# Four graph layers on one core: sharing single tiles of exponentials between ScalarE and VectorE

## The chip, the core and the metric

The kernel runs on one core of a Trainium2 chip. TensorE (PE in the profile) multiplies matrices, ScalarE (ACT) evaluates functions such as the exponential, VectorE (DVE) does elementwise arithmetic and reductions, GpSimd (POOL) copies and starts some of the transfers, SyncE (SP) starts most of them. The engines run side by side and wait for each other through semaphores. Matrix products land in PSUM, a small memory of eight banks; everything else lives in SBUF. The metric is device time of one execution in microseconds (us).

## What is computed

Four layers follow each other on a graph of N = 3327 nodes with D = 128 features. Nearly all of the time is in the first, an attention with 128 "heads" (one for each of the d = 128 rows of the reshaped q, k and v) of depth 8, whose scores get the adjacency matrix added twice:

```python
q = (x @ Wq.T).reshape(d, n, h)          # d = 128, n = 3327, h = 8; k and v alike
a = jnp.einsum('dnh,dmh->dnm', q, k) * d ** -0.5
a = a + adj + adj
a = jax.nn.softmax(a, axis=2)
out = jnp.einsum('dnm,dmh->dnh', a, v).reshape(n, h * d) @ Wo.T
x = layernorm(x + out)
```

So 128 x 3327 x 3327 exponentials are needed. The other layers are products with the adjacency matrix: one scaled by the inverse roots of its row sums, one with rows divided by row sums plus the transpose divided by column sums, and one plain, each with a residual and a layer norm.

## The kernel before

**Tiling of the attention.** The queries are cut into seven columns of CW = 476, the keys into 26 tiles of 128, and these into four key blocks KBS of 7, 7, 6 and 6 tiles, called here kb 0 to 3. A block of work is one column with one key block: 28 blocks, taken column by column with kb 0 to 3 inside. In a block the 128 heads d run in 32 groups of four (GROUP).

**One step.** For one head, `exponents` (line 616) is called three times, for the three sets of SETS: 3, 2 and 2 key tiles where the block has 7, and 2, 2 and 2 where it has 6. A set si has score banks `sc[si]` of its own (3 + 2 + 2 of PSUM's 8 banks). TensorE writes one 128 x 476 product for each tile (line 632; the added adjacency comes in through the operands), then an engine reads the whole set out of PSUM and writes the exponentials to `e` in SBUF. That is ScalarE with one activation for the set (line 640), except for the last set of a group's first head in most groups (`on_vector`, line 454): that whole set is done on VectorE by `vector_exp` (line 590). Over the kernel 784 sets of two tiles go to VectorE, 9,968 to ScalarE.

**The exponential on VectorE.** Line 596 reads PSUM, clamps, and scales into an integer whose upper bits are an exponent. Lines 597 and 599 split it by bit operations into a power of two and a mantissa. Five operations of line 602 then evaluate a polynomial of degree five (Horner's rule, the last one multiplies by the power). The first of these eight is issued at once, the others are kept in the list `vec`.

**The weighing.** One group later, `weigh` (line 647) multiplies the exponentials with the values: for one key tile r, four heads side by side, summed over the key block in the eighth bank `o`. PLACES, FIRST and FULL say after which of the twelve sets of a group each of the 6 or 7 weighings stands. After three groups `flush` (line 665) adds `o` into `acc` on VectorE.

**Order.** The attention is written with a manual schedule: the order of instructions on TensorE, ScalarE, GpSimd and VectorE is that of the program text. VectorE's kept operations are placed by `vector_work` (line 607), which has a clock for ScalarE (0.95 or 0.84 for each set) and one for VectorE, and takes operations from `vec` as long as VectorE's clock is behind. In a spare moment the adjacency matrix is transposed in 91 pieces of 512 x 256 (`piece_work`, line 213), whose row sums and column sums are taken on VectorE too: a transpose and three reductions, in two bursts, in every eighth group. `copy_queries` (line 513) prepares the next group's queries on VectorE where kb is 0.

**After the attention.** `divide` (line 1119) normalises with GpSimd, and three gathers (`gather`, line 1098) multiply the transposed adjacency, loaded as one 128 x 26 x 128 tile `eT` for each row tile through a pool of five buffers, with the features.

Of the kernel before, what the change touches and what calls it, by code (L numbers as in the profile page):

```python
# [30 lines left out]
POLY = (-0.12145248055458069, 1.287218689918518, 0.8447736501693726, 0.7106341123580933, 0.24892811477184296)  # L31
# [19 lines left out]
def kernel(ctx: ExitStack, tc: tile.TileContext, x, adj, wq, wk, wv, wo,  # L51
# [83 lines left out]
    colsum = const.tile([P, T], F32, name="colsum")  # L135
# [20 lines left out]
    csum = const.tile([P, NP // 32], F32, name="csum")  # L156
# [56 lines left out]
    def piece_work(pool, u, c, ai):  # L213

        nj = PIECE // 32
        w = min(PIECE, N - c * PIECE)
        at = pool.tile([P, nj, 4, 32], F32, name="at")
        nc.vector.transpose(at.rearrange("p j t b -> p t j b"), ai.rearrange("p t (j a) -> p t j a", a=32))
        yield at
        if c == 0:  # L220
            maxima[u] = pool.tile([P, 4, NPC], F32, name="pmax")
            sums[u] = pool.tile([P, 4, NPC], F32, name="psum")
        nc.vector.tensor_reduce(maxima[u][:, :, c], ai[:, :, 0:w], AX.X, ALU.max)
        yield at
        nc.vector.tensor_reduce(sums[u][:, :, c], ai[:, :, 0:w], AX.X, ALU.add)
        yield at
        part = csum[:, c * nj:(c + 1) * nj]
        if u == 1:
            nc.vector.tensor_reduce(part, at.rearrange("p j t b -> p j (t b)"), AX.X, ALU.add)
        else:  # L230
            cs = pool.tile([P, nj], F32, name="cs")
            nc.vector.tensor_reduce(cs, at.rearrange("p j t b -> p j (t b)"), AX.X, ALU.add)
            nc.vector.tensor_tensor(part, part, cs, ALU.add)
        yield at

    def store_tops(pool, u, top, n):

        hi = pool.tile([P, 4], F32R, name="rhi")
        nc.vector.tensor_copy(hi, top)
        lo = pool.tile([P, 4], F32R, name="rlo")  # L240
        nc.vector.tensor_tensor(lo, top, hi.bitcast(F32), ALU.subtract)
        for row, sb in enumerate((hi, lo)):
            for i in range(P // n):
                nc.gpsimd.dma_start(out=flat_ap(lead_s[u], row * SUPER + i * P, [[1, n], [n, 4]]),
                                    in_=sb[n * i:n * i + n, :].bitcast(F32))
# [172 lines left out]
    def attention():  # L418
        with tc.tile_pool(name="ed", bufs=1) as ed, tc.tile_pool(name="kq", bufs=3) as kq, \
# [34 lines left out]
            def on_vector(kb, g):  # L454

                return g % 4 != 0 if kb == 0 else KBS[kb][1] == 7 or g % 8 != 0
# [5 lines left out]
            PLACES = {7: (1, 1, 4, 6, 8, 10, 10), 6: (0, 2, 4, 6, 8, 10)}  # L462
# [79 lines left out]
            loaded, worked, turning = [], [], []  # L542

            def background(n):
                if n % PACE == 2 and worked:
                    piece_store(pe, *worked.pop(0))
                if n % PACE == 2 and pieces:
                    u, c = pieces.pop(0)
                    loaded.append((u, c, piece_load(pe, u, c)))

            def background_work(n):
                if n % PACE == 4 and loaded:
                    u, c, ai = loaded.pop(0)
                    steps = piece_work(pe, u, c, ai)
                    worked.append((u, c, next(steps)))
                    next(steps)
                    clock[1] += 2.4
                    turning.append(steps)
                if n % PACE == 0 and turning:
                    clock[1] += 2.4  # L560
                    for _ in turning.pop():
                        pass

            def prepare(b, d):

                n = b * NHG + d // GROUP
                if d % GROUP == 0:
                    while any(of is None for _, of, _ in vec):
                        vec.pop(0)[2]()
# [12 lines left out]
                if n + 1 < len(groups) and blocks[groups[n + 1][0]][1] == 0 \  # L582
                        and d % GROUP == 1 - on_vector(blocks[b][1], d // GROUP):
# [6 lines left out]
            def vector_exp(e, x, of):  # L590


                y = ex.tile([P, 2, CW], F32, name="ey")
                t = ex.tile([P, 2, CW], F32, name="et")
                yi, ti = y.bitcast(I32), t.bitcast(I32)
                nc.vector.tensor_scalar(yi, x, -58 * math.log(2.0), 2 ** 24 / math.log(2.0), ALU.max, ALU.mult)  # L596
                vec.append((0.7, of, lambda: nc.vector.tensor_scalar(ti, yi, UPPER, EXPONENT, ALU.bitwise_and,  # L597
                                                                 ALU.bitwise_xor)))
                vec.append((0.7, of, lambda: nc.vector.tensor_scalar(yi, yi, LOWER, QUARTER, ALU.bitwise_and,  # L599
                                                                 ALU.bitwise_or)))  # L600
                for i, a in enumerate(POLY):
                    vec.append((1.2, of, lambda i=i, a=a: nc.vector.scalar_tensor_tensor(  # L602
                        e, e if i else y, a, t if i == len(POLY) - 1 else y, ALU.add, ALU.mult)))

            clock = [0.0, 0.0]

            def vector_work(b):

                while vec and clock[1] < clock[0]:
                    cost, _, step = vec.pop(0)  # L610
                    step()
                    clock[1] += cost
                clock[0] += 0.95 if KBS[blocks[b][1]][1] == 7 else 0.84
                clock[1] = max(clock[1], clock[0] - 1)

            def exponents(b, d, si):
# [19 lines left out]
                if on_vector(kb, d // GROUP) and (d % GROUP, si) == (0, 2):  # L636
                    vector_exp(e[:, 0:n, :], s[:, 0:n, 0:CW], (b, d // GROUP))
                    clock[1] += 1.2
                else:
                    nc.scalar.activation(e[:, 0:n, :], s[:, 0:n, 0:CW], AF.Exp, scale=2.0)  # L640
# [6 lines left out]
            def weigh(b, g, r):  # L647
# [6 lines left out]
                while any(of == (b, g) for _, of, _ in vec) and r >= SETS[len(queue_of)][2][0]:  # L654
                    vec.pop(0)[2]()
# [19 lines left out]
            def store(b, f):  # L675
                nb = min(PACK, NHG - f * PACK)
                for j in range(GROUP):
                    nc.gpsimd.dma_start(  # L678
# [6 lines left out]
            with tc.manual_schedule(engines={mybir.EngineType.PE, mybir.EngineType.Activation,  # L685
# [8 lines left out]
                for b, d in steps:  # L694
# [3 lines left out]
                    for si in range(len(SETS[KBS[blocks[b][1]][1]])):  # L698
                        vector_work(b)
# [335 lines left out]
    pick = act.tile([P, 32], F32, name="pick")  # L1035
    nc.vector.tensor_tensor(pick, ident[:, 0:32], ident[:, 32:64], ALU.add)
    nc.vector.tensor_tensor(pick, pick, ident[:, 64:96], ALU.add)
    nc.vector.tensor_tensor(pick, pick, ident[:, 96:128], ALU.add)
    ps = bank(7)
    nc.tensor.matmul(ps[0:32, 0:NP // 32], lhsT=pick, rhs=csum, start=True, stop=True)  # L1040
    for q in range(4):
        nc.vector.tensor_copy(colsum[32 * q:32 * q + 32, :],
                              ps[0:32, 0:NP // 32].rearrange("a (s q) -> a q s", q=4)[:, q, :])

# [17 lines left out]
    inv_col = inverse_degree(colsum, "inv_col")  # L1062
# [34 lines left out]

    def gather(t, y, col, b, meanwhile=()):
# [13 lines left out]
        for _, what in todo:  # L1112
            what()
        return ps
# [4 lines left out]
    def divide(t):  # L1119
# [7 lines left out]
        nc.gpsimd.tensor_tensor(ons[t][:n], o[:n, 0:H, :], rec[:n, :].unsqueeze(1).to_broadcast([n, H, D]), ALU.mult)  # L1127
# [38 lines left out]
    with tc.manual_schedule(engines={mybir.EngineType.PE, mybir.EngineType.SP}):  # L1166
# [18 lines left out]
        for t in range(T):  # L1185
# [9 lines left out]
            norm(n, h[:n, :], xs[1][:n, t, :])  # L1195

# [77 lines left out]
```

## Time and profile before

| what | value |
|---|---|
| time, median of 3 runs | 10,740.89 us (10,740.8 to 10,744.52) |
| the profiled execution | 10,739.45 us, its span 10,737.5 us |
| first to last exponential on ScalarE | 317.7 to 9,966.2 us |
| from there to the end | 771 us |
| ScalarE's activations, line 640 | 9,968, busy 9,360.0 us |
| VectorE's polynomial steps, line 602 | 3,920, busy 4,511.6 us |
| column sums, lines 229, 232 and 233 | busy 123.4 us |

The profile gives, for each engine, the time that its instructions took and, for each group of instructions, the idle time of the engine ahead of them and the instruction whose semaphore ended it. Busy times of the engines overlap: the share of one engine says nothing on the path. A matmul's end is modelled, so that a busy TensorE isn't one at its peak; the distance between the starts of its instructions says more. On ScalarE an activation's record lasts longer than its share of the pipeline: the next one starts 844 ns after a two-tile set and 1,241 ns after a three-tile set where nothing holds it up (medians of start to start), though their records last 1,016 and 1,402 ns on average.

### The profile page before, as it was taken

What the parts mean: (1) busy time and instruction counts of PE and PEld (TensorE: products, weight loads), DVE (VectorE), ACT (ScalarE), POOL (GpSimd) and SP (SyncE); (2) the same over time, 40 slices, a digit from 0 to 9 for tenths busy, and PEclk for the clock granted to TensorE, in tenths of its full rate; (3) what the DMA queues carried; (4) which work ended last, traced back from release to release, by engine and by line L of the source; (5) the groups of instructions that cost most, each with busy time, mean ns of one, the idle gap of its engine ahead of it and who ended that gap; (6) DMA issues with size and microseconds to landing.
All of it is one profiled execution on the core that took longest, in us unless ns stands there. A gap on an engine that the chain in (4) does not pass through costs nothing. (4 is left out here: it accounts for less than half of the span.)

```text
span 10737.5 us, 200822 instructions
## 1 busy us (share of the span) xinstructions
PE 10565.1 (98%) x76941; PEld 4105.8 (38%) x76941; DVE 7960.2 (74%) x8554; ACT 9584.8 (89%) x10447; POOL 1554.7 (14%) x2739
## 2 busy tenths in 40 slices
PE   8899999999999999999999999999999999999999
PEld 5333333333333333333333333333333333333779
DVE  6777888777888777887788777888777777777412
ACT  3899999999999999999999999999999999999400
POOL 0111121111221111211122110121111100001200
PEclk9999999999999999999999999999999999999999
DMA  7678886788876888768887588886888867788676
GB/s 270 181 184 188 209 210 181 181 192 201 213 188 171 198 201 209 190 166 200 198 211 196 156 191 191 199 199 172 193 195 202 193 162 179 181 189 196 219 283 246
DMA packets 1013760, 2116.43 MB, mean 197 GB/s; under 512 B 206759, under 2 KB 730985, under 8 KB 998979
## 3 DMA queue, kind: packets, MB, share of 16 engines
q1 hardware_dynamic: 932014, 1985.55, 74.4%
q0 software_dynamic: 79392, 116.16, 3.5%
q8 instruction: 623, 10.21, 0.4%
q14 instruction: 335, 2.74, 0.1%
q10 hardware_dynamic: 1396, 1.77, 0.1%
HBM read 1863.03 MB, written 239.54 MB: 196 GB/s over the span
## 5 line engine op out<-in xcount | busy, mean ns | idle before, releaser
L640 ACT ACTIVATE e<-sc 128x952 f32<-128x952 f32 (+1 forms) x9968 | 9360.0, 1085 | 312.1 <-PE sc L632 284.3
L658 PE MATMUL o<-e,v_pad 128*32 128x476 f32 (+1 forms) x46592 | 5647.1, 573 | 39.4 <-DVE acc L671 18.5
L632 PE MATMUL sc<-qt,kt 64*128 64x476 f32 x23296 | 4491.6, 440 | 52.9 <-ACT e L640 33.5
L632 PEld LDWEIGHTS sc<-qt,kt 64*128 64x128 f32 x23296 | 2184.3, 184 | 4433.6 <-ACT e L640 3740.6
L602 DVE SCALAR_TENSOR_TENSOR e<-e,ey 128x952 f32<-128x952 f32 x2352 | 2707.0, 1151 | 77.4
L596 DVE TENSOR_SCALAR ey<-sc 128x952 int32<-128x952 f32 x784 | 901.1, 1149 | 1411.5 <-PE sc L632 1389.9
L658 PEld LDWEIGHTS o<-e,v_pad 128*32 128x32 f32 (+1 forms) x46592 | 1035.2, 108 | 1907.4 <-issue 1885.1
L533 POOL COPY v_pad<-vs 128x192 f32<-128x192 f32 (+1 forms) x896 | 444.5, 522 | 8018.6 <-DMA vs<-v_img 6214.0
L602 DVE SCALAR_TENSOR_TENSOR e<-ey 128x952 f32<-128x952 f32 x784 | 903.4, 1152 | 27.2
L602 DVE SCALAR_TENSOR_TENSOR e<-e,et 128x952 f32<-128x952 f32 x784 | 901.2, 1149 | 22.3
L253 POOL DMA_DIRECT2D adjT_s<-at x1352 | 760.1, 570 | 132.7 <-DMA adjT_s<-at 92.6
L599 DVE TENSOR_SCALAR ey<-ey 128x952 int32<-128x952 int32 x784 | 519.7, 663 | 27.1
L597 DVE TENSOR_SCALAR et<-ey 128x952 int32<-128x952 int32 x784 | 518.3, 661 | 26.9
L1110 PE MATMUL bank<-y,eT 128*128 128x128 f32 (+1 forms) x4056 | 473.9, 276 | 0.4 <-DVE h L1232 0.4
L1110 PEld LDWEIGHTS bank<-y,eT 128*128 128x128 f32 (+1 forms) x4056 | 465.3, 192 | 5.7 <-DVE h L1232 0.6
L671 DVE TENSOR_TENSOR acc<-o,acc 128x476 f32<-128x476 f32 x231 | 150.3, 651 | 281.5 <-PE o L658 280.9
L517 DVE TENSOR_SCALAR qt<-qt 32x1428 fp32r<-32x1428 f32 x224 | 201.7, 900 | 103.2 <-DMA qt<-q_s 89.2
L519 DVE CAST qt<-qt 64x1904 fp32r<-64x1904 f32 x224 | 260.4, 1163 | 7.6
L1070 ACT ACTIVATE rstd<-mv,eps 128x1 f32<-128x1 f32 x104 | 30.4, 292 | 263.6 <-DVE mv L1068 263.6
L678 POOL DMA_DIRECT2D o_s<-acc x308 | 199.4, 651 | 35.4 <-DVE acc L671 20.8
L1213 PE MATMUL bank<-a,y 128*128 128x512 f32 (+2 forms) x364 | 145.5, 562 | 0.0
L362 ACT ACTIVATE hi<-pp 128x1024 fp32r<-128x1024 f32 x52 | 53.0, 1024 | 87.9 <-PE pp L308 86.3
(148 smaller groups left out, 2274.7 us busy)
## 6 DMA issues: line engine op xcount, KB each, us to landing
qt<-qimg SPq DMA_DIRECT2D x1344, 476.0 KB
kt<-k_s SPq DMA_DIRECT2D x5316, 96.0 KB
kt<-k_s SPq DMA_DIRECT2D x1762, 128.0 KB
eT<-adjT_s SPq DMA_DIRECT2D x78, 1664.0 KB
qimg<-qt SPq DMA_DIRECT2D x224, 476.0 KB
vs<-v_img SPq DMA_DIRECT2D x224, 224.0 KB
adjT_s<-at POOLq DMA_DIRECT2D x1352, 32.0 KB, 4.8
vs<-v_img SPq DMA_DIRECT2D x224, 192.0 KB
```

The lines of the kernel that those rows point to most:

```text
L253: nc.gpsimd.dma_start(out=flat_ap(adjT_s, (t * P + 32 * q) * NP + c * PIECE, [[NP, 32], [P, ns], [1, P]]), in_=at[32 * i:32 * i + 32].rear ...
L517: return [(0.9, None, lambda: nc.vector.tensor_scalar(qt[32:64, 1:], qf[0:32, 0:GROUP - 1], -1.0, None, ALU.mult)), (0.4, None, lambda: nc ...
L519: (1.2, None, lambda: nc.vector.tensor_copy(qt[64:128], qf[0:64]))]
L533: nc.gpsimd.tensor_copy(vp[:, 32:32 + nt * GROUP * 32].rearrange("p (x c) -> p x c", c=32)[:, :, 0:H], vs.rearrange("p (x c) -> p x c", c=H))
L596: nc.vector.tensor_scalar(yi, x, -58 * math.log(2.0), 2 ** 24 / math.log(2.0), ALU.max, ALU.mult)
L597: vec.append((0.7, of, lambda: nc.vector.tensor_scalar(ti, yi, UPPER, EXPONENT, ALU.bitwise_and, ALU.bitwise_xor)))
L599: vec.append((0.7, of, lambda: nc.vector.tensor_scalar(yi, yi, LOWER, QUARTER, ALU.bitwise_and, ALU.bitwise_or)))
L602: vec.append((1.2, of, lambda i=i, a=a: nc.vector.scalar_tensor_tensor(e, e if i else y, a, t if i == len(POLY) - 1 else y, ALU.add, ALU.m ...
L632: nc.tensor.matmul(s[:, i, 0:CW], lhsT=kt[64 * rg:64 * rg + 64, k, pos * P:(pos + 1) * P], rhs=qt[64 * rg:64 * rg + 64, k, :], start=False ...
L640: nc.scalar.activation(e[:, 0:n, :], s[:, 0:n, 0:CW], AF.Exp, scale=2.0)
L658: nc.tensor.matmul(o[32 * j:32 * j + 32, 0:CW], lhsT=values[b, g][:m, c:c + 32], rhs=es[b, g * GROUP + j, r][:m, :], start=(r == 0 and u = ...
L1110: nc.tensor.matmul(ps[:n, 0:D], lhsT=e[:m, s, :n], rhs=y[:m, s, col:col + D], start=(s == 0), stop=(s == T - 1))
```

## The change

Where VectorE took a whole set of two tiles, it now takes the second tile of twice as many sets; ScalarE does the other tile of such a divided set, and its activation is issued first. 1,554 sets are divided (48, 64, 55 and 55 in a block of kb 0, 1, 2 and 3), all spaced evenly: every 6th set in kb 1, about every 7th in kb 2 and 3. The polynomial has one coefficient fewer; both engines' exponentials carry a common factor, which PHASE sets and which the division takes out again. `vector_exp` keeps all but its first operation in `vec` as before, now 476 wide and with two buffers each for `y` and `t`. The two clocks get a cost for each size of activation, and VectorE's operations are taken only up to the time at which its next fixed duty (a divided set, or a flush) is due. The background work comes in three single steps that are taken where they fit. In 6-tile blocks the weighings stand after sets 1, 3, ..., 11 in place of 0, 2, ..., 10. Column sums are no longer taken from the pieces: in the second layer's gather each loaded `eT` is reduced and summed (`add_columns`). The very last stores of the attention go through the SyncE and ScalarE queues, and the first `divide` multiplies on VectorE.

```diff
-POLY = (-0.12145248055458069, 1.287218689918518, 0.8447736501693726, 0.7106341123580933, 0.24892811477184296)
+POLY = (-0.039287679561190725, 0.7694055213858888, 0.3602062482980112, 0.1471829588776368)
+PHASE = 0.7927868171488225 * math.log(2.0) / 2
...
         nc.vector.tensor_reduce(sums[u][:, :, c], ai[:, :, 0:w], AX.X, ALU.add)
         yield at
-        part = csum[:, c * nj:(c + 1) * nj]
-        if u == 1:
-            nc.vector.tensor_reduce(part, at.rearrange("p j t b -> p j (t b)"), AX.X, ALU.add)
-        else:
-            cs = pool.tile([P, nj], F32, name="cs")
-            nc.vector.tensor_reduce(cs, at.rearrange("p j t b -> p j (t b)"), AX.X, ALU.add)
-            nc.vector.tensor_tensor(part, part, cs, ALU.add)
-        yield at
...
-            def on_vector(kb, g):
-                return g % 4 != 0 if kb == 0 else KBS[kb][1] == 7 or g % 8 != 0
+            def on_vector(b, d, si):
+                kb = blocks[b][1]
+                p = 3 * d + si
+                if kb == 0:
+                    return p % 24 in (2, 11, 17)
+                if KBS[kb][1] == 7:
+                    return p % 6 == 2
+                return p % 7 == 2 and p % 12 != 9 or p % 7 == 3 and p % 12 == 10
...
-            PLACES = {7: (1, 1, 4, 6, 8, 10, 10), 6: (0, 2, 4, 6, 8, 10)}
+            PLACES = {7: (1, 1, 4, 6, 8, 10, 10), 6: (1, 3, 5, 7, 9, 11)}
...
+            def background(n):
+                if spare:
+                    return
...
                     steps = piece_work(pe, u, c, ai)
-                    worked.append((u, c, next(steps)))
-                    next(steps)
-                    clock[1] += 2.4
-                    turning.append(steps)
-                if n % PACE == 0 and turning:
-                    clock[1] += 2.4
-                    for _ in turning.pop():
-                        pass
+                    spare.extend([lambda: worked.append((u, c, next(steps))), lambda: next(steps), lambda: next(steps)])
...
             def vector_exp(e, x, of):
-                y = ex.tile([P, 2, CW], F32, name="ey")
-                t = ex.tile([P, 2, CW], F32, name="et")
+                while sum(to is not None for _, to, _ in vec) > len(POLY):
+                    take()
+                y = ex.tile([P, CW], F32, name="ey", bufs=2)
+                yi, parts = y.bitcast(I32), {}
                 nc.vector.tensor_scalar(yi, x, -58 * math.log(2.0), 2 ** 24 / math.log(2.0), ALU.max, ALU.mult)
...
-                    vec.append((1.2, of, lambda i=i, a=a: nc.vector.scalar_tensor_tensor(
-                        e, e if i else y, a, t if i == len(POLY) - 1 else y, ALU.add, ALU.mult)))
+                    vec.append((0.69, of, lambda i=i, a=a: step(i, a)))
...
-            def vector_work(b):
-                while vec and clock[1] < clock[0]:
-                    cost, _, step = vec.pop(0)
-                    step()
-                    clock[1] += cost
-                clock[0] += 0.95 if KBS[blocks[b][1]][1] == 7 else 0.84
-                clock[1] = max(clock[1], clock[0] - 1)
+            COST = (0.0, 0.455, 0.85, 1.265)
+            def next_fixed(b, d, si):
+                at, nt = clock[0], KBS[blocks[b][1]][1]
+                for _ in range(12):
+                    if on_vector(b, d, si):
+                        return at + COST[SETS[nt][si][1] - 1] + 0.15
+                    if 3 * (d % GROUP) + si == 11 and (d // GROUP % PACK == PACK - 1 or d == D - 1):
+                        return at + 0.3
+                    at += COST[SETS[nt][si][1]]
+                    ...
+            def vector_work(b, d, si):
+                until = next_fixed(b, d, si)
+                if spare and clock[1] + sum(cost for cost, _, _ in vec) + 1.2 <= until + 0.2 and clock[1] < clock[0] + 0.9:
+                    spare.pop(0)()
+                    clock[1] += 1.2
+                while vec and clock[1] + vec[0][0] <= min(until, clock[0] + 2.4):
+                    take()
+                clock[1] = max(clock[1], clock[0] - 0.3)
...
-                if on_vector(kb, d // GROUP) and (d % GROUP, si) == (0, 2):
-                    vector_exp(e[:, 0:n, :], s[:, 0:n, 0:CW], (b, d // GROUP))
-                    clock[1] += 1.2
-                else:
-                    nc.scalar.activation(e[:, 0:n, :], s[:, 0:n, 0:CW], AF.Exp, scale=2.0)
+                own = n - on_vector(b, d, si)
+                nc.scalar.activation(e[:, 0:own, :], s[:, 0:own, 0:CW], AF.Exp, bias=-2 * PHASE, scale=2.0)
+                clock[0] += COST[own]
+                if own < n:
+                    vector_exp(e[:, own, :], s[:, own, 0:CW], (b, d // GROUP, t0 + own))
+                    clock[1] = max(clock[1], clock[0] + 0.1) + 0.68
...
-                while any(of == (b, g) for _, of, _ in vec) and r >= SETS[len(queue_of)][2][0]:
-                    vec.pop(0)[2]()
+                while any(of is not None and of[0:2] == (b, g) and of[2] <= r for _, of, _ in vec):
+                    take()
...
-                    nc.gpsimd.dma_start(
+                    (nc.gpsimd if not last else (nc.sync, nc.scalar)[j % 2]).dma_start(
...
-    ps = bank(7)
-    nc.tensor.matmul(ps[0:32, 0:NP // 32], lhsT=pick, rhs=csum, start=True, stop=True)
...
+    def add_columns(t):
+        part = colsum if t == 0 else small.tile([P, T], F32, name="part")
+        nc.vector.tensor_reduce(part, eTs.pop(t), AX.X, ALU.add)
+        if t:
+            nc.vector.tensor_tensor(colsum, colsum, part, ALU.add)
...
-        nc.gpsimd.tensor_tensor(ons[t][:n], o[:n, 0:H, :], rec[:n, :].unsqueeze(1).to_broadcast([n, H, D]), ALU.mult)
+        (nc.gpsimd if t else nc.vector).tensor_tensor(ons[t][:n], o[:n, 0:H, :], rec[:n, :].unsqueeze(1).to_broadcast([n, H, D]), ALU.mult)
...
             norm(n, h[:n, :], xs[1][:n, t, :])
+            add_columns(t)
+        inv_col = inverse_degree(colsum, "inv_col")
```

## The prediction

> **What bounds the kernel now.** I read the busy shares first, then the groups by form, the windows of one block of each kind, and last the timelines of ScalarE and TensorE in them. The page's part 1 (busy us, share of the span):
>
> ```profile
> PE 10565.1 (98%) x76941; PEld 4105.8 (38%) x76941; DVE 7960.2 (74%) x8554; ACT 9584.8 (89%) x10447; POOL 1554.7 (14%) x2739
> ```
>
> TensorE seems full and ScalarE close behind. Groups by form (busy us, mean ns of one | idle before, releaser):
>
> ```profile
> L640 ACT ACTIVATE e<-sc 128x952 f32<-128x952 f32 x8176 | 7323.8, 1016 | 193.8 <-PE sc L632 189.7
> L602 DVE SCALAR_TENSOR_TENSOR e<-e,ey 128x952 f32<-128x952 f32 x2352 | 2707.0, 1151 | 77.4
> L640 ACT ACTIVATE e<-sc 128x1428 f32<-128x1428 f32 x1792 | 2512.5, 1402 | 118.2 <-PE sc L632 94.6 <-DMA kt<-k_s 23.6
> L596 DVE TENSOR_SCALAR ey<-sc 128x952 int32<-128x952 f32 x784 | 901.1, 1149 | 1411.5 <-PE sc L632 1389.9 <-ACT e L640 19.6
> L597 DVE TENSOR_SCALAR et<-ey 128x952 int32<-128x952 int32 x784 | 518.3, 661 | 26.9
> L671 DVE TENSOR_TENSOR acc<-o,acc 128x476 f32<-128x476 f32 x231 | 150.3, 651 | 281.5 <-PE o L658 280.9
> ```
>
> ScalarE waits for nothing but scores. VectorE stands 1,411 us before line 596: it has room. Windows of blocks of kb 0, 1, 2 and 3 (start:end, length, then busy us and count of PE, PEld, DVE, ACT, POOL):
>
> ```profile
> 3070.20:3438.60 368.40, 360.76 (x2710) 129.28 (x2708) 299.71 (x319) 363.91 (x361) 60.45 (x104) 1.00 0.67 173
> 3438.60:3807.10 368.50, 367.21 (x2718) 130.69 (x2716) 287.92 (x292) 356.24 (x353) 54.91 (x106) 1.00 0.84 194
> 3807.10:4127.40 320.30, 319.12 (x2339) 105.38 (x2337) 253.69 (x256) 308.37 (x357) 50.26 (x97) 1.00 0.86 205
> 4127.40:4447.20 319.80, 318.28 (x2330) 105.06 (x2328) 255.12 (x258) 308.77 (x357) 74.08 (x132) 1.00 0.85 207
> ```
>
> Timeline of ScalarE in the kb 2 block (start, us, count, idle before):
>
> ```profile
> 4002.73 9.53 ACT L640 ACTIVATE e<-sc 128x952 f32<-128x952 f32 x11 [0.32 <-PE sc L632]
> 4012.55 9.53 ACT L640 ACTIVATE e<-sc 128x952 f32<-128x952 f32 x11 [0.29 <-PE sc L632]
> 4022.38 9.53 ACT L640 ACTIVATE e<-sc 128x952 f32<-128x952 f32 x11 [0.30 <-PE sc L632]
> ```
>
> One line is one group: eleven activations without a break, then a wait, at the set that VectorE takes. A group lasts 9.82 us, and 11 starts at 844 ns are 9.28: 0.54 idle. TensorE in the same group:
>
> ```profile
> 4002.14 0.81 PE L632 MATMUL sc<-qt,kt 64*128 64x476 f32 x4
> ...
> 4003.81 0.70 PE L632 MATMUL sc<-qt,kt 64*128 64x476 f32 x4
> ...
> 4005.39 0.69 PE L632 MATMUL sc<-qt,kt 64*128 64x476 f32 x4
> ...
> 4006.95 0.70 PE L632 MATMUL sc<-qt,kt 64*128 64x476 f32 x4
> ...
> 4008.51 1.02 PE L632 MATMUL sc<-qt,kt 64*128 64x476 f32 x4
> ...
> 4010.40 0.69 PE L632 MATMUL sc<-qt,kt 64*128 64x476 f32 x4
> ```
>
> Between starts it needs 1.56 to 1.58 us for two sets and a weighing, but 1.67 and 1.89 once each. Six times 1.566 is 9.40: it loses 0.42 in a group, though the records show it busy. So two nearly equal stations take turns waiting. Between VectorE's sets ScalarE (0.844 a set) falls behind TensorE (0.783), till TensorE finds no free bank; then VectorE takes a whole set at once and ScalarE has nothing to read.
>
> **What the Trainium skill says.** "Trainium Kernel Development and Optimization", section Performance Expectations, calls matmul busy time a bad metric, because matmuls are pipelined; the trace agrees (98% busy, 0.42 of 9.82 us lost). "ScalarE: Activation LUTs", What ACT_TABLE_LOAD costs: 186 ns plus 0.833 an element with immediate scale and bias, 93 more for each pointer operand, 93 of overlap back to back. The new bias is an immediate in the built program, so the 93 stay away from 10,752 activations (they would be 1.0 ms). "VectorE: DVE Perf Modes", Mode 2×_2P — use both read ports for one tensor: a single-source fp32 operation from SBUF runs at two elements a cycle, from PSUM at one; the trace has 661 against 1,149 ns.
>
> **The change part by part.** Starts of consecutive records give 844 ns for two tiles and 1,241 for three.
>
> Idle of ScalarE today. From 317.7 to 9,966.2 us are 9,648.5; 8,176 x 0.844 + 1,792 x 1.241 = 9,125 is work; 523 is waiting. By place: 419 within 2.5 us of VectorE's sets (58 in kb 0, 120 in kb 1, 240 in kb 2 and 3: 0.35, 0.54 and 0.61 for each of 168, 224 and 392 sets), 57 at block starts, 24 at the first load, the rest scattered. Only the 419 is in play.
>
> Divided sets, ScalarE. VectorE gets 1,554 tiles instead of 1,568. ScalarE runs 1,792 three-tile, 7,406 two-tile and 1,554 one-tile activations. One tile isn't in the trace: 0.844 less the step 1.241 - 0.844 gives 0.447; by the skill's page 93 + 397 = 490 ns. I take 0.447: 2,224 + 6,251 + 695 = 9,170, so +45; at 0.490 +112.
>
> Divided sets, waiting. A whole set freed 0.844 and left 0.61 idle in 6-tile blocks, so 0.23 was absorbed; 0.31 in kb 1, 0.49 in kb 0. Half a set frees 0.397, which leaves 0.17, 0.09 and nothing. But the built program lets VectorE's read of PSUM wait for ScalarE's half: the shortest records of two and three tiles are 952 and 1,348 ns, so one tile ends after about 556, then some 100 of signalling and 650 of reading follow: the bank is free 1.3 us after ScalarE's start, against 1.0 for a full set. In 6-tile blocks half of the divided sets stand first of a pair, and the bank's next user follows after 1.57 + 0.32 us; there TensorE may lose 0.1 to 0.3. Against that, even spacing lets ScalarE fall behind by only 0.06 x 7 = 0.42 before it catches up. I take 0.15 for the 770 sets of kb 2 and 3, 0.08 for the 448 of kb 1, 0.03 for the 336 of kb 0: 116 + 36 + 10 = 162. Bounds: 0 if all is absorbed; 0.41 if 0.29 of later release adds to 0.12 everywhere.
>
> VectorE. Old chain for two tiles: 1,149 + 661 + 663 + 5 x 1,151 = 8.23 us, 4.11 a tile. New widths aren't in the trace; line 671, 476 wide, has 651, and halving 661 above a fixed 160 gives 0.41: 0.65 + 2 x 0.41 + 4 x 0.655 = 4.09. The fourth polynomial step saved pays for the fixed cost of narrow operations. 1,554 x 4.09 = 6,356 against 6,451, and 123 of column sums go too: VectorE keeps a quarter free in the attention. Were this cover gone, each late read would hold a bank. Queued behind a waiting first operation are the other steps of `vec`; 3.5 us of work; the weighing that needs the tile is at least seven sets (5.5 us) away, by the places in the text.
>
> Background pieces, `copy_queries`, weighings after sets 1 to 11: same operations, GpSimd's 1,352 and SyncE's piece transfers moved with them, hidden behind the attention; zero.
>
> Tail. `add_columns` costs a reduction of 3,328 elements (3,616 ns for 3,327 at line 411) and 0.17: 3.8 us in a gather period of 6.35, beside 1.5 us of VectorE's own work (39.66 us busy from 10,093 to 10,250 us, over 26): fits, but the small add stands in the chain to the next transpose, which has about 0.2 to spare: 0 to +5. Held one period longer, `eT` still has four of its five buffers. The last stores leave GpSimd, whose four issues took 2.35 us, and the first `divide` needn't wait for GpSimd (it started at 9,988.4, its input was there at 9,981.3; the second tile still waits): -3 to -10. Net -5.
>
> Sum: -419 + 45 + 162 - 5 = -217. On the profiled execution's 10,739.45 (span 10,737.5 plus 2) that is 10,522; the median is 1.4 above it, which is within rounding: 10,520.
>
> **Rivals.**
> - All absorbed: both stations run at ScalarE's pace. -419 + 45 - 10 = -384, 10,355. For: 6-tile blocks then take 302, TensorE's 6 x 32 x 1.566 = 301 allows it. Against: two equal stations with three sets of banks absorb only what they did (0.23).
> - TensorE is the bound as its 98% says, and 1.67 and 1.89 are its own: no change, 10,735. Against: all other steps are 1.56 to 1.58, and its weight loads wait for line 640.
> - Slower: the hand-over from ScalarE to VectorE to TensorE in the divided sets. If the later release (0.29) comes on top of 0.12 at each of 1,554 sets, -419 + 45 + 637 - 5 = +258, 10,997. It decides from a mean wait of 0.24 us on: (419 - 45 + 5)/1,554. For: VectorE can't read before ScalarE has finished, and a reduction of 1.2 us ahead of it makes it later. Against: most banks have 2 us and more before their next use.
>
> **How the numbers follow.** Forecast 0.62, all absorbed (under 10,430) 0.22, no change 0.05, slower 0.11. Range: mean waits of 0.01 to 0.22 at a divided set give 10,376 to 10,702, rounded outward below; the dearer price of one tile (+67) lies within. Outside are the slower rival, no change and the lower end of the second case, together about 0.2. 0.2% is 21 us, what can be told from no change here: faster 0.84, same 0.05, slower 0.11.
>
> **What would show it.** Right: one-tile starts at 0.45; ScalarE's waits at divided sets near 0.1 in place of 0.6; blocks of 363, 357 and 313 us for kb 0, 1 and 2; TensorE's 1.89 steps gone; the tail at 766. Wrong: weight loads of line 632's successor waiting for the new integer operation on VectorE by hundreds of us, or 6-tile blocks still at 320.

## The result: slower by 3.9%

The changed kernel takes 11,160.8 us (median of 4 runs, 11,156.0 to 11,174.0), the kernel before 10,742.7 beside it: a ratio of 1.0391, 95% interval [1.0373, 1.0409]. The forecast was 10,520. The profiled execution has a span of 11,172.0 us. From the first to the last exponential there are now 10,012.8 us (9,648.5 before, +364), from there to the end 840.0 (771.3, +69). Line numbers in the views are those of each run's own kernel. Part 1 of the page after (busy us, share of the span):

```profile
PE 10558.4 (95%) x76939; PEld 4036.4 (36%) x76939; DVE 7837.6 (70%) x13036; ACT 9709.9 (87%) x11231; POOL 1518.0 (14%) x2734
```

Every engine is busy for nearly as long as before, TensorE, VectorE and ScalarE with smaller shares: little was added to work on, something is waited for. The groups by form (busy us, mean ns of one | idle before):

```profile
L659 ACT ACTIVATE e<-sc 128x952 f32<-128x952 f32 x7406 | 6801.4, 988 | 376.4 <-PE sc L654 317.2 <-issue 7.7 <-ACT e L659 1.3
L595 DVE SCALAR_TENSOR_TENSOR e<-e,ey 128x476 f32<-128x476 f32 x3108 | 2040.0, 656 | 102.5
L588 DVE TENSOR_SCALAR ey<-sc 128x476 int32<-128x476 f32 x1554 | 1016.0, 654 | 2252.9 <-ACT e L659 2252.4
L659 ACT ACTIVATE e<-sc 128x476 f32<-128x476 f32 x1554 | 933.0, 600 | 117.9 <-PE sc L654 117.1
L592 DVE TENSOR_SCALAR et<-ey 128x476 int32<-128x476 int32 x1554 | 636.9, 410 | 45.6
L694 DVE TENSOR_TENSOR acc<-o,acc 128x476 f32<-128x476 f32 x231 | 148.9, 645 | 4.7 <-PE o L681 4.7
```

The new widths cost what the forecast took (654, 410 and 656 ns), and the next activation starts 447 ns after a one-tile one (median where nothing is waited for). ScalarE's work, by starts of 447, 844 and 1,241 ns, is 9,169 us, as foretold. But of 10,012.8 us this leaves 844 idle, where 524 were before. The last row is `flush`. Before, VectorE stood 281 us waiting for the weighing's bank; now 4.7. So VectorE comes to the flush late: the median time from the end of a weighing to the flush that adds it up was 0.07 us before and is 1.08 now. Windows of the blocks of kb 0 to 3 in the third column:

```profile
3179.00:3563.10 384.10, 361.45 (x2712) 132.68 (x2708) 295.17 (x458) 366.80 (x384) 60.03 (x104) 1.00 0.65 167
3563.10:3937.50 374.40, 365.01 (x2719) 130.87 (x2717) 278.77 (x472) 360.33 (x385) 57.46 (x107) 1.00 0.84 189
3937.50:4273.10 335.60, 317.62 (x2339) 96.81 (x2337) 243.35 (x409) 314.57 (x385) 47.70 (x97) 0.99 0.86 195
4273.10:4607.80 334.70, 316.67 (x2332) 96.50 (x2328) 246.12 (x411) 313.49 (x385) 69.78 (x132) 0.99 0.85 199
```

All four kinds are longer, by 15.7, 5.9, 15.3 and 14.9 us, where 5 to 12 less was foretold. The last three columns are the granted clock, the share of the DMA engines and GB/s. The clock is 0.99 to 1.00 and the share within 0.02 of before, so neither the clock nor the transfers explain blocks that are 6 to 16 us longer. ScalarE in the kb 2 block:

```profile
3984.39 29.78 ACT L659 ACTIVATE e<-sc 128x952 f32<-128x952 f32 x36 [1.30 <-PE sc L654]
4015.42 29.68 ACT L659 ACTIVATE e<-sc 128x476 f32<-128x476 f32 x36 [1.25 <-PE sc L654]
4045.84 14.99 ACT L659 ACTIVATE e<-sc 128x952 f32<-128x952 f32 x18 [0.74 <-PE sc L654]
```

The wait of 0.3 us in every group is gone, as hoped; shorter ones don't show in this view (see the hand-over below). A long one comes every 36 activations: twelve sets times three groups, the distance from one flush to the next. TensorE and VectorE at one of them, in a kb 3 block:

```profile
4314.46 1.01 PE L681 MATMUL o<-e,v_pad 127*32 127x476 f32 x8
...
4314.92 0.66 DVE L595 SCALAR_TENSOR_TENSOR e<-ey 128x476 f32<-128x476 f32 x1
...
4315.61 1.34 DVE L595 SCALAR_TENSOR_TENSOR e<-e,ey 128x476 f32<-128x476 f32 x2
...
4316.87 0.65 DVE L694 TENSOR_TENSOR acc<-o,acc 128x476 f32<-128x476 f32 x1
...
4317.66 1.01 PE L681 MATMUL o<-e,v_pad 128*32 128x476 f32 x8 [1.56 <-DVE acc L694]
...
4319.13 3.38 ACT L659 ACTIVATE e<-sc 128x952 f32<-128x952 f32 x4 [1.31 <-PE sc L654]
```

The last weighing of three groups ends at 4,315.5. The flush could start, but two polynomial steps stand ahead of it on VectorE (1.34 us). There is one bank `o`; TensorE's next weighing waits 1.56 us for it with the scores queued behind, and ScalarE runs dry for 1.31. Waits of TensorE and of VectorE, whole run (us in all, times, longest):

```profile
PEld sc L654 <- DVE ey L588: 552.0, 905, 1.9
...
PE o L681 <- DVE acc L694: 241.1, 207, 1.9
...
DVE part L1114 <- DMA eT<-adjT_s: 55.1, 19, 6.1
...
PE bank L1099 <- DVE x L1091: 43.3, 12, 4.9
...
PE o L681 <- DVE acc L692: 30.9, 38, 0.8
```

Waits of a weighing for a flush: 241.1 + 30.9 = 272 us. Before, they were 30:

```profile
PE o L658 <- DVE acc L671: 18.5, 38, 1.5
...
PE o L658 <- DVE acc L669: 11.1, 34, 1.1
```

The first line, score banks held by VectorE's first operation, was 204.1 before; with what is put down to VectorE's other operations it is 826 now and was 485. The third and fourth belong to the tail, where the chain of waits (start, us) reads:

```profile
10570.74 7.09 DMA eT<-adjT_s
10577.85 3.62 DVE part L1114
10584.04 2.99 PE bank L1132 x14
10587.88 2.08 PE bank L1132 x14
10589.97 6.62 DMA eT<-adjT_s
10596.61 3.62 DVE part L1114
```

Before, a row tile of this gather took 6.35 us, set by the matmuls. Now the load of the next `eT` and the reduction of it stand on the chain too, and two tiles take 19 us.

### The profile page after: what moved, and what is told of

Read it like the earlier page. It is cut to its first block, busy times and chain, and to the rows that moved or that the text cites. A ratio compares the mean times of both kernels' runs of the same rounds, so it can differ in the third digit from the quotient of the medians.

```text
span 11172.0 us, 205846 instructions
## 1 busy us (share of the span) xinstructions
PE 10558.4 (95%) x76939; PEld 4036.4 (36%) x76939; DVE 7837.6 (70%) x13036; ACT 9709.9 (87%) x11231; POOL 1518.0 (14%) x2734
## 5 line engine op out<-in xcount | busy, mean ns | idle before, releaser
L659 ACT ACTIVATE e<-sc 128x952 f32<-128x952 f32 (+2 forms) x10752 | 9486.9, 999 | 551.5 <-PE sc L654 481.5
L681 PE MATMUL o<-e,v_pad 128*32 128x476 f32 (+1 forms) x46592 | 5685.2, 576 | 291.4 <-DVE acc L694 241.1
L654 PE MATMUL sc<-qt,kt 64*128 64x476 f32 x23296 | 4409.3, 436 | 200.2 <-ACT e L659 120.1
L654 PEld LDWEIGHTS sc<-qt,kt 64*128 64x128 f32 x23296 | 2080.7, 185 | 4493.1 <-ACT e L659 3306.0
L588 DVE TENSOR_SCALAR ey<-sc 128x476 int32<-128x476 f32 x1554 | 1016.0, 654 | 2252.9 <-ACT e L659 2252.4
L595 DVE SCALAR_TENSOR_TENSOR e<-e,ey 128x476 f32<-128x476 f32 x3108 | 2040.0, 656 | 102.5
L595 DVE SCALAR_TENSOR_TENSOR e<-e,et 128x476 f32<-128x476 f32 x1554 | 1021.1, 657 | 51.1
L595 DVE SCALAR_TENSOR_TENSOR e<-ey 128x476 f32<-128x476 f32 x1554 | 1019.0, 656 | 53.9
L599 DVE TENSOR_SCALAR ey<-ey 128x476 int32<-128x476 int32 x1554 | 641.7, 413 | 53.8
L592 DVE TENSOR_SCALAR et<-ey 128x476 int32<-128x476 int32 x1554 | 636.9, 410 | 45.6
L1114 DVE TENSOR_REDUCE part<-eT 128x26 f32<-128x3328 f32 x25 | 90.4, 3617 | 55.2 <-DMA eT<-adjT_s 55.1
```

The lines of the kernel that those rows point to most:

```text
L592: nc.vector.tensor_scalar(parts["t"].bitcast(I32), yi, UPPER, EXPONENT, ALU.bitwise_and, ALU.bitwise_xor)
L595: nc.vector.scalar_tensor_tensor(e, e if i else y, a, parts["t"] if i == len(POLY) - 1 else y, ALU.add, ALU.mult)
L599: vec.append((0.41, of, lambda: nc.vector.tensor_scalar(yi, yi, LOWER, QUARTER, ALU.bitwise_and, ALU.bitwise_or)))
L654: nc.tensor.matmul(s[:, i, 0:CW], lhsT=kt[64 * rg:64 * rg + 64, k, pos * P:(pos + 1) * P], rhs=qt[64 * rg:64 * rg + 64, k, :], start=False ...
L659: nc.scalar.activation(e[:, 0:own, :], s[:, 0:own, 0:CW], AF.Exp, bias=-2 * PHASE, scale=2.0)
L681: nc.tensor.matmul(o[32 * j:32 * j + 32, 0:CW], lhsT=values[b, g][:m, c:c + 32], rhs=es[b, g * GROUP + j, r][:m, :], start=(r == 0 and u = ...
```

## The experiments

My theory after the profile: three losses, the flush, the reduction in the tail, and the hand-over from ScalarE to VectorE in a divided set. The rivals were that one of them makes all of it, and that the moved weighings or the narrower work are to blame. Times are medians; "attention" is first to last exponential in the profile.

| run | us | ratio [95%] | attention |
|---|---|---|---|
| e1_flush_seen | 10,905.0 | 1.0154 [1.0137, 1.0171] | 9,749.4 |
| e2_no_columns | 11,092.1 | 1.0331 [1.0314, 1.0348] | 10,001.0 |
| e3_whole_sets | 10,764.7 | 1.0025 [1.0015, 1.0034] | 9,601.4 |
| e4_old_places | 11,163.7 | 1.0395 [1.0377, 1.0412] | 10,002.7 |
| e5_flush_tail | 10,837.8 | 1.0083 [1.0068, 1.0099] | 9,750.7 |
| e6_own_banks | 10,799.3 | 1.0051 [1.0036, 1.0066] | 9,701.5 |
| e7_one_tile | 10,931.4 | 1.0174 [1.0158, 1.0189] | 9,833.4 |
| e8_whole_tail | 10,715.1 | 0.9973 [0.9962, 0.9983] | 9,626.1 |
| e9_kb0_single | 10,866.1 | 1.0112 [1.0095, 1.0129] | 9,778.7 |
| e10_kb0_as_kb1 | 10,768.2 | 1.0023 [1.0015, 1.0031] | 9,675.0 |
| e11_whole_single | 10,782.2 | 1.0034 [1.0022, 1.0047] | 9,696.8 |
| e12_all_mended | 10,708.5 | 0.9974 [0.9963, 0.9984] | 9,613.1 |
| e13_last_at_11 | 10,887.6 | 1.0141 [1.0124, 1.0158] | 9,797.8 |

### The flush

`next_fixed` keeps VectorE free for set 11 of a group whose number leaves 2 when divided by 3. But weighing runs one group behind: the flush of that pack is issued in the next group, after its last weighing. The time kept free is one group early.

```diff
-                    if 3 * (d % GROUP) + si == 11 and (d // GROUP % PACK == PACK - 1 or d == D - 1):
+                    if flush_after(b, d, si):
                         return at + 0.3
+            def flush_after(b, d, si):
+                g = d // GROUP
+                prev, pb = (g - 1, b) if g else (NHG - 1, b - 1)
+                if pb < 0 or not (prev % PACK == PACK - 1 or prev == NHG - 1):
+                    return False
+                n = KBS[blocks[pb][1]][1]
+                last = (FIRST[n] if g == 0 else PLACES[n] if blocks[b][1] else FULL[g % 4])[-1]
+                return 3 * (d % GROUP) + si == last
```

> The clocks keep VectorE free ahead of the set after which the flush really stands (the reservation of the changed kernel names the last set of a group in which no flush falls). Theory A, flush: TensorE's wait for acc falls from 272 us to under 60, the attention from 10,013 to about 9,780 us, the time to 10,900 to 10,950. Theory B, hand-over in the divided sets: the waits for acc fall but come back at the score banks, and the time falls by less than 60 us, to 11,100 or more.

Measured: 11,160.8 - 10,905.0 = 256 us gained by an edit that moves VectorE's operations and adds none. ScalarE's idle time falls from 844 to 580. The same place in a kb 2 block, and the wait:

```profile
3925.08 1.01 PE L690 MATMUL o<-e,v_pad 128*32 128x476 f32 x8
...
3926.16 0.65 DVE L703 TENSOR_TENSOR acc<-o,acc 128x476 f32<-128x476 f32 x1 [0.48 <-PE o L690]
...
3926.96 1.01 PE L690 MATMUL o<-e,v_pad 128*32 128x476 f32 x8 [0.23 <-DVE acc L703]
```

```profile
PE o L690 <- DVE acc L703: 43.2, 136, 1.3
```

VectorE now waits for the weighing, as before (0.07 us from a weighing's end to the flush), and TensorE hardly for VectorE. By medians a block gains 2.4, 8.3, 13.4 and 13.2 us in kb 0 to 3. The flush is the largest single loss.

### The tail

> Leaves out the column sums (add_columns; the row sums stand in for them), so the tail is without the 26 reductions. Theory C, reductions queued on VectorE ahead of the norm and waiting for the next eT: the part after the last exponential falls from 840 to about 770 us, the time by 65 to 75 to about 11,090, the attention stays at 10,013. If the tail's loss has another origin (transfers, stores), it stays at 840.

```diff
-            add_columns(t)
-    colsum = act.tile([P, T], F32, name="colsum")
-        inv_col = inverse_degree(colsum, "inv_col")
+        inv_col = inverse_degree(rowsum, "inv_col")
```

e2 leaves the column sums out. The time from the last exponential to the end fell from 840.0 to 769.6, the total by 69 us. To learn whether the sums are cheaper in the attention, e5 has e1's edit and takes them from the pieces again, in a fourth single step, with the `pick` product of before at the end.

> The flush foreseen as in the first experiment, and the column sums back in the background pieces (a fourth single step), none in the tail. If flush and tail are separate losses they add: 10,905 - 69 is 10,836, at most 25 more for the 123 us of reductions that VectorE has again in the attention. The tail after the last exponential is 765 to 775 us. If VectorE has no room for the reductions beside divided sets, the attention grows by 60 or more.

```diff
+        part = csum[:, c * nj:(c + 1) * nj]
+        if u == 1:
+            nc.vector.tensor_reduce(part, at.rearrange("p j t b -> p j (t b)"), AX.X, ALU.add)
...
+        yield at
...
-            add_columns(t)
```

67 us less than e1; the tail is 767.2 and the attention the same (9,750.7 against 9,749.4). With a free quarter of VectorE the sums cost nothing there. Both mends add up: 256 + 67 = 323 of the 418 us that the change lost.

### Weighings after odd sets

> Weighings of 6-tile blocks after sets 0, 2, ..., 10 again, all else as changed. Theory A: the flush is due one set earlier and is as little foreseen; the wait for acc and the time change by less than 60 us. Theory B: the divided sets that stand first of a pair become second and the other way round, half of each in both cases: no change. If the places themselves cost, the 6-tile blocks fall from 335 towards 320 us and the time by up to 200.

```diff
-            PLACES = {7: (1, 1, 4, 6, 8, 10, 10), 6: (1, 3, 5, 7, 9, 11)}
+            PLACES = {7: (1, 1, 4, 6, 8, 10, 10), 6: (0, 2, 4, 6, 8, 10)}
```

3 us longer, inside the interval: the places of the 6-tile blocks are neither loss nor gain beside the rest.

### Whole sets under the new rules

> VectorE takes whole sets in the groups of the kernel before, with the new polynomial, clocks, places and tail. Theory A: the reservation still misses the flush, TensorE waits for acc as long as now (200 us or more), the attention stays within 100 of 10,013. Theory B: the loss goes with the divided sets, the attention falls to 9,700 or less and the time to about 10,850.

```diff
+                kb, g = blocks[b][1], d // GROUP
+                if (d % GROUP, si) != (0, 2):
+                    return False
+                return g % 4 != 0 if kb == 0 else KBS[kb][1] == 7 or g % 8 != 0
```

VectorE takes whole sets of two again, in the old groups, with one buffer for each of `y` and `t` and the clocks' costs to match; the shorter polynomial, the scheduling by clocks, places and tail stay as in the change. The attention takes 9,601 us, 47 less than before: all of the loss in the attention comes with the dividing. (How the 47 are shared between polynomial, clocks and background steps isn't separated.) The wrong reservation does no harm here: TensorE waits 15.3 us for flushes, and VectorE 467.2 for the weighing. Its chain, begun at the third set of a group, is over when the flush comes. With the sums back in the pieces (e8) this is faster than both kernels:

> Whole sets on VectorE as before the change, with the new polynomial, clocks and places, and the column sums back in the pieces. If losses add: 10,765 - 69 is 10,696, up to 10,715 with the reductions: below the kernel before by 0.2 to 0.4%. If the clocks alone gave the attention's 30 us, their gain is gone with the fuller VectorE and the time is 10,740 or more.

10,715.1 us, 0.9973 [0.9962, 0.9983].

### The hand-over

The two banks of the third set were one tile, and a dependency holds for the tile: VectorE's read waits for ScalarE's half though it reads another bank. e6 makes two tiles of them, so that it waits for TensorE alone. Only third sets are divided (in 6-tile blocks 55 of 64 p with p % 6 = 2), and undivided third sets take two one-tile activations: 2,030 more (12,782 against 10,752; the expectation's 2,548 is too many), each 447 + 447 - 844 = 50 ns, about 101 us of ScalarE's work. e7 is its control, with the same sets and activations, and one tile.

```diff
-            sc = [psc.tile([P, n, 512], F32, name=f"sc{i}") for i, n in enumerate((3, 2, 2))]
+            sc = [psc.tile([P, n, 512], F32, name=f"sc{i}") for i, n in enumerate((3, 2))]
+            sc.append([psc.tile([P, 1, 512], F32, name=f"sc2{i}") for i in range(2)])
...
+                if si == 2:
+                    for i in range(own):
+                        nc.scalar.activation(e[:, i, :], s[i][:, 0, 0:CW], AF.Exp, bias=-2 * PHASE, scale=2.0)
...
-                    vector_exp(e[:, own, :], s[:, own, 0:CW], (b, d // GROUP, t0 + own))
+                    vector_exp(e[:, own, :], bank_of(si, s, own)[:, 0:CW], (b, d // GROUP, t0 + own))
```

> As the run before, but the two banks of the third set are separate tiles, so that VectorE's read waits for TensorE alone and not for ScalarE's half; divided sets are third sets only (48, 64, 55, 55 in a block as before), and undivided third sets take two activations of one tile. To be compared with the control of the next run, which has the same divided sets and activations in one tile. Theory B, hand-over ScalarE to VectorE to TensorE: at least 100 us below the control, most of it in the blocks of kb 0. Theory D, the places of the divided sets among the weighings, not the hand-over: within 40 us of the control.

> Control of the run before: same divided sets, same single activations for undivided third sets, the two banks in one tile, so that VectorE's read waits for ScalarE's half. The added activations (2,548 times about 0.044 us) cost up to 112 us of ScalarE's time: 10,840 to 10,960.

132 us between the two. VectorE's first operation in e7 and in e6 (waits):

```profile
DVE ey L598 <- ACT e L679: 1791.4, 1500, 6.3
PEld sc L673 <- DVE ey L598: 428.2, 936, 2.3
```

```profile
DVE ey L599 <- PE sc L677: 1260.2, 937, 7.4
```

The wait for ScalarE is gone, and with it the weight loads' wait for VectorE. But the gain isn't where it was expected, in kb 0. A kb 1 and a kb 2 block of e7, then of e6:

```profile
3509.40:3879.40 370.00, 367.47 (x2719) 131.27 (x2717) 284.78 (x476) 362.97 (x449) 51.67 (x98) 1.00 0.82 191
3879.40:4204.80 325.40, 320.73 (x2338) 96.89 (x2337) 241.67 (x412) 320.16 (x459) 42.53 (x82) 1.00 0.84 198
```

```profile
3479.80:3849.20 369.40, 367.42 (x2719) 131.94 (x2717) 282.75 (x479) 362.79 (x449) 48.78 (x97) 1.00 0.82 192
3849.20:4165.00 315.80, 313.61 (x2339) 97.52 (x2337) 238.95 (x409) 313.04 (x458) 40.84 (x83) 1.00 0.87 204
```

9.6 us a block in kb 2 and the like in kb 3, 14 blocks, makes all of it; kb 1 gains 0.6, kb 0 nothing (382.5 and 382.4, medians). Summed by place from the starts of ScalarE's activations, its waits in kb 2 and 3 at the set four behind the divided one fall from 130 us to 8. TensorE lost its time at the set three behind, which uses the same banks: there its weight loads wait 239 us for VectorE's read in e7 and not at all in e6. ScalarE felt it one set later. Separate tiles also free the first bank of an undivided third set earlier. That seems to give little: at the set four behind such a set ScalarE's waits are 14 us in e7 and 11 in e6.

"PSUM — Partial Sum Buffer", section PSUM bank collisions raise a hardware error, says that two engines must not touch one bank in the same 32 partitions at once, while different banks run clean. The tiles of one set lie in different banks, so the wait in the change came from the one tile, not from the chip. The trace agrees: in e6 1,085 of VectorE's 1,554 reads overlap the one-tile activation of their set by more than 0.2 us, none does in e7, and a read takes 652 ns against 654.

### The weighings of kb 0

With flush and tail mended, kb 0's blocks still took 382.6 us (367.3 with whole sets). ScalarE's waits stood before fixed sets, counted from 0 over the 48 sets of four groups: on average 0.64 us before set 13, 0.59 before 20 and 0.50 before 37 (the expectation below counts one more, 14, 21 and 38), each right behind a pair of weighings that FULL places.

```diff
-            FULL = ((0, 2, 4, 4, 7, 7, 9), (0, 0, 3, 7, 7, 10, 10), (0, 0, 3, 6, 6, 9, 9), (0, 0, 3, 6, 7, 10, 10))
+            FULL = ((1, 1, 4, 6, 8, 10, 10),) * 4
```

> As e5_flush_tail (10,837.8 us, kb 0 blocks 382.6 us), only the weighings of kb 0 are moved: one after each of sets 1, 2, 4, 6, 8, 9, 11 of every group, where FULL had pairs after sets 0, 4, 6, 7, 9 or 10. Theory A, the places: FULL's pairs were set to fall on the moments at which VectorE took a whole set; with the divided sets elsewhere ScalarE runs dry behind each pair. Then ScalarE's waits at sets 14, 21 and 38 (0.5 to 0.6 us each) go, kb 0's seven blocks take 368 to 374 us in place of 382.6 and the time is 10,740 to 10,780. Theory B, the hand-over or something else about divided sets in kb 0: blocks stay within 2 us of 382.6 and the time within 15 us of e5. Blocks of kb 1, 2 and 3 stay at 366.7, 322.1 and 321.3 either way.

> As e9_kb0_single, but with the places that kb 1 uses, pairs after sets 1 and 10 and single ones after 4, 6, 8. Theory A: a pair in a group still runs ScalarE dry where no divided set or slack covers it, so that kb 0's blocks come out between e9's and 382.6, about 373 to 379 us, and the time is 10,770 to 10,815. Theory B: unchanged at 382.6 us and 10,838.

> Control for the places: e8_whole_tail (whole sets, 10,715 us, kb 0 blocks 367.3 us) with the weighings of kb 0 spread as in e9. Theory A: FULL was made for whole sets, so that taking it away costs something here, kb 0's blocks 368 to 376 us and 10,720 to 10,775. Theory B, that FULL's pairs are bad by themselves: kb 0's blocks under 365 us and a time under 10,700.

e10's edit is shown; e9 has (1, 2, 4, 6, 8, 9, 11), and so has e11, on e8's whole sets. The same kb 0 block in e5 and e10:

```profile
3102.20:3486.30 384.10, 364.62 (x2712) 133.38 (x2708) 301.07 (x468) 366.40 (x384) 60.39 (x104) 0.99 0.64 166
```

```profile
3079.00:3449.50 370.50, 365.36 (x2712) 131.00 (x2708) 300.78 (x468) 364.39 (x384) 58.30 (x104) 1.00 0.66 173
```

The expectation on single weighings was wrong: e9 is longer than e5, by 28 us, with new waits of 0.41 to 0.60 us before set 3 of each group. Pairs of weighings as such aren't to blame. But kb 1's places take 12 us from a block of kb 0 by medians (10 on average, 70 in all), with the same sets divided. Against single weighings FULL is worth 10 us a block to whole sets (367.3 and e11's 377.2) and 3 to divided ones (382.6 and 385.4). So what a table of places is worth depends on the sets that VectorE takes; the change moved the sets and left FULL. Whether kb 1's places would have helped whole sets in kb 0 too is open: that wasn't run.

### Why kb 0 and kb 1 don't gain, and all four together

> As e10_kb0_as_kb1 (10,768 us; kb 0's blocks 370.6, kb 1's 365.9), with one of the seven weighings of kb 0 and kb 1 moved: 1, 1, 4, 6, 8, 10, 11 in place of 1, 1, 4, 6, 8, 10, 10. In e10 ScalarE waits 0.38 to 0.40 us at the first set of each group, behind the pair of weighings after set 10, where whole sets gave 0.5 us behind VectorE's set. Theory A, that pair is what keeps the blocks of kb 1 at 366 us instead of the 357 foretold: the wait at set 0 goes, kb 1's blocks take 354 to 361 us, kb 0's 360 to 366, the time is 10,620 to 10,700. Theory B, TensorE has no room for it (98% busy) and the wait comes back behind another weighing, at set 3 or 4: blocks within 3 us of e10's, the time 10,745 to 10,790, or longer if three weighings close together (11, 1, 1) are worse than the pair.

```diff
-            7: (1, 1, 4, 6, 8, 10, 10)
+            7: (1, 1, 4, 6, 8, 10, 11)
```

In kb 1, e10 still has 0.40 us of wait before set 11 of each group, right behind the pair of weighings after set 10 (the expectation puts it one set later). With one of the two moved by one set that wait goes, but others come behind the new places: 0.32 us before set 0 in kb 1 and 0.25 in kb 0, and 0.24 and 0.43 before set 2. Weighings after sets 11, 1 and 1 stand close together. kb 1's blocks take 372.6 us in place of 365.9, kb 0's 382.7 in place of 370.6. What would remove the waits of the 7-tile blocks stays open.

> The four losses found so far mended together: the reservation for the flush, the column sums in the pieces, kb 0's weighings at kb 1's places (all as in e10_kb0_as_kb1, 10,768 us), and the third set's banks as separate tiles (as in e6_own_banks, 10,799 us, which still had FULL in kb 0). Theory A, the losses are these four and add up: 10,799 - 70 = 10,729, between 10,710 and 10,745, kb 0's blocks at 368 to 372 us, kb 1's 366 to 370, those of kb 2 and 3 at 315 to 316; the undivided third sets, done as two activations, cost about 101 us of ScalarE's work in it. Theory B, they overlap: 10,750 to 10,800.

10,708.5 us, 0.9974 [0.9963, 0.9984], a little better than the sum of the parts (10,729). Its blocks of kb 0 to 3:

```profile
3068.10:3439.80 371.70, 364.85 (x2712) 130.78 (x2708) 301.05 (x467) 367.64 (x465) 59.15 (x104) 1.00 0.65 173
3439.80:3809.30 369.50, 367.56 (x2719) 131.94 (x2717) 282.59 (x479) 362.72 (x449) 50.45 (x97) 1.00 0.80 191
3809.30:4125.10 315.80, 313.61 (x2339) 97.49 (x2337) 238.84 (x409) 313.05 (x458) 41.20 (x83) 1.00 0.85 204
4125.10:4440.40 315.30, 312.55 (x2333) 97.04 (x2329) 241.63 (x417) 312.90 (x458) 66.29 (x123) 1.00 0.86 207
```

The four losses make up the slowdown, and more: mended, the divided sets beat the kernel before by 0.26%, though ScalarE has 101 us more to do than in the change. Its idle time in the attention is 342 us (524 before). e12 and e8 can't be told apart; either is the version to keep.

## Why the prediction was wrong

**Where it failed.** "Queued behind a waiting first operation are the other steps of `vec`; 3.5 us of work; the weighing that needs the tile is at least seven sets (5.5 us) away". Two of VectorE's duties were named, the read of the scores and the finished tile. The third, the flush, is in the same queue and holds the only bank of sums. It had no term in the sum; it cost 256 us. "VectorE keeps a quarter free in the attention" was true (70% busy) and no cover: the free time lies ahead of the first operation of each chain, where VectorE waits (2,252 us), and the flush comes inside the chain. "PSUM — Partial Sum Buffer", section Engine vs sequencer instructions, says that VectorE's queue is strict first-in, first-out; the flush at 4,316.87, 1.4 us after its input was complete, agrees.

**"Fits" in the tail.** A net of -5 was foretold, +69 came. Without the reductions (e2) the tail is 1.7 us shorter than before, so the rest of it did little of its -3 to -10. The reduction was sized well (3,617 ns for 3,616), and a period of 6.35 us with 1.5 of other work has room for it on average. But it waits for the load of `eT`, and on VectorE it stands ahead of `z`, `h` and the norm of a tile already complete. The program text has `add_columns` behind the norm, but the manual schedule of this part covers TensorE and SyncE alone, and in the built order the reductions run ahead: three start before the first `z` (the third at 10,453.3 us, `z` at 10,456.8). TensorE's transpose waits for the norm (43.3 us), and the loads wait for TensorE to finish a tile (193.5 us between 10,430 and 10,690; 5.8 for a reduction): a ring of load, reduction, norm and product.

**The wait at a divided set.** The mechanism was right, and the slower rival was built on it: the bank is free 1.29 us after ScalarE's start (600 + 33 + 654 ns), where 1.3 was reckoned, though the "100 of signalling" in it is 33. 162 us was allowed, of it 116 for kb 2 and 3; with e7's sets the shared tile costs 132, all there. The size was fair, the spread wrong: nothing in kb 0, where 10 was allowed, and next to nothing in kb 1, where 36 was. The rival's price (637) was far too high: the slowdown it foretold came, but mainly from other causes, and that it named the right outcome was luck.

**What was to go.** Of the 419 us at VectorE's sets, taken as "in play", little went in the 7-tile blocks. With all four losses mended, e12 has 371.7 and 369.5 us in kb 0 and 1 against 363 and 357 foretold (e10 370.6 and 365.9), and only kb 2 comes to 315.8, near the 313. Waits behind weighings took the old waits' place. I had read the end of the wait, "VectorE takes a whole set at once and ScalarE has nothing to read", as its cause; e10 and e13 show that where the weighings stand decides as much.

**"Background pieces, `copy_queries`, weighings after sets 1 to 11": zero.** The places of the 6-tile blocks are zero (e4). That kb 0's places were left as they were cost about 70.

**What held.** The durations of all new widths, ScalarE's +45, and VectorE's chain for a tile (4.10 us for 4.09). Weight loads "waiting for the new integer operation on VectorE by hundreds of us", named as a sign of failure, came (552.0), but that line isn't the measure of the loss: in e1 it stays (576.6) while 256 us go, and from e7 to e6 423 us of it go for 132 of time.

## What to carry to other kernels

Before giving an in-order engine smaller and more frequent portions, list everything else in its queue, and for each the buffer that it holds and how many there are: a 0.65 us duty with a single bank, behind two short steps, cost 256 us, more than the whole rearrangement was forecast to gain (217). Free time on average is no cover for a duty with a moment of its own; a schedule that reserves time by a clock has to be checked in the trace against where that duty stands. Tables of places made for one division of work have to be tried anew for another.

## What the runs showed of the hardware

A one-tile activation (476 elements from PSUM, immediate scale and bias) lets the next start after 447 ns, not the 490 that can be estimated from "ScalarE: Activation LUTs", What ACT_TABLE_LOAD costs (186 + 397 less 93); the measurement decides: one, two and three tiles are 50 ns plus 397 each. VectorE's narrow read of PSUM takes 652 ns in e6, mostly with ScalarE reading the neighbouring bank beside it, and 654 in the change, with ScalarE's half finished first.
